# Layer 0's attention to the context: keys and values projected in the self-attention before it, batches in a pipeline

## The chip, the cores and the metric

One core of a Trainium2 chip runs the whole program. Its engines work from queues of their own, each in order: TensorE (PE; its weight loads are listed as PEld), VectorE (DVE), ScalarE (ACT), GpSimd (POOL) and SyncE (SP, which here only starts transfers). The metric is the device time of one execution in microseconds; the time before is 2743.05 us, the median of three runs (2738.83 to 2749.72).

## What is computed

The reference is a decoder of four layers on 8 batches of 256 tokens with 256 features, each layer made of a part that mixes the tokens (in layer 0 a self-attention), an attention to a context (8 batches of 120 rows with 192 features) and a feed-forward part, each followed by an addition and a layer norm. The parts of the first three layers stand one after the other in the list `LAYERS`; the fourth layer is run from inside the third's feed-forward part, and the change does not touch it. Only these lines of the reference matter here:

```python
x = _layernorm(x + _L0_attn_ref(x, ...))
x = _layernorm(x + _L0_xattn_ref(x, ctx_768, Wq, bq, Wk, bk, Wv, bv))

def _L0_xattn_ref(image_features, text_features, Wq, bq, Wk, bk, Wv, bv):
    query = jnp.einsum('bqi,ih->bqh', image_features, Wq) + bq
    key = jnp.einsum('bkt,th->bkh', text_features, Wk) + bk
    value = jnp.einsum('bkt,th->bkh', text_features, Wv) + bv
    scale = 1.0 / jnp.sqrt(jnp.asarray(HID, query.dtype))
    scores = jnp.einsum('bqh,bkh->bqk', query, key) * scale
    weights = jax.nn.softmax(scores, axis=-1)
    return jnp.einsum('bqk,bkh->bqh', weights, value)
```

The attention to the context has one head of 256 features and no output projection. Its keys and values depend on the context alone, so they do not wait for the self-attention.

## The kernel before

`Net` keeps the tokens in `X` (128 tokens per tile, 16 tiles, two per batch), a transposed copy in `xT` (features on the partitions), and the transposed context in `ctxT`. `build` runs the parts in order, and loads each part's weights one part ahead: `load` (L120, L124) takes one of two slots in turn, and starts the transfers on SP's queue. A part's slot is therefore free for the load after the next only when that part is through with it. The program's instructions are placed on the engines' queues by a scheduler which may move them past each other where the data allow it; on the chip each queue then runs in its order.

`l0_attn` works in turns of `t`, 0 to 7. In each turn `exps` and `largest` make score products in four banks at a time (`four_banks`, mask L443, scores L448), `lower16` turns the row maxima (L500) and writes them into the queries (L502), `sums` multiplies the exponentials with the values (L275), and `divided16` divides. Every even turn `pair` projects queries, keys and values of the next two. All of it takes PSUM banks from one rotation of eight (`bank`): six of the pool `sc`, then the two of the transposes, `pt`. After the turns, `project_out` runs for the eight batches: product with `wo` (L134), addition (L292), then `finish`: statistics on VectorE (L165, L166), the reciprocal root on GpSimd (`rsqrt`, L143 and L145, since `power` is set for this part), X on VectorE (L189), and four transposes with a copy on ScalarE back into `xT` (L175, L176).

`l0_xattn` opens pools of its own and projects first: keys for all 960 context rows (`project_T`, evicted at L334), queries for all 2048 tokens (the same lines, scaled by 1/16), values per batch with the bias as a third product (L136) and a copy on ScalarE (L360). Then it runs over 8 batches with two halves each: score product, negative row maximum (L371), exponential with its sum (L374), reciprocal (L375), transpose of the weights into `pt` (L377), its copy (L379), product with the values, division and addition in one (L382). `finish` closes the batch.

`l0_ffn` comes next. It makes the router's 32 small products with `xT` (`plog`), copies them (L827), finds each token's expert, writes X to memory (L877, on ScalarE's queue; the scheduler starts each write as soon as its X is there), and then gathers the experts' weights and rows.

A product in 32-bit floats shows as two rows, called passes here, each with a weight load of its own.

Of the kernel before, what the change touches and what calls it, by code (L numbers as in the profile page):

```python
# [11 lines left out]
F32 = mybir.dt.float32  # L12
# [30 lines left out]
class Net:  # L43
# [169 lines left out]
    def l0_attn(self, w):  # L213
# [3 lines left out]
        nc = self.nc  # L217
        wq, wk, wv, wo, bv, bo = w
        rows = [slice(32 * r, 32 * r + 32) for r in range(4)]
        of = [slice(0, P), slice(P, 2 * P)]  # L220
        xs = self.xT.rearrange("p c (g n) -> p c g n", n=P)
        with ExitStack() as ctx:
            work, low, vps = self.attn16_pools(ctx, "a0", P, 2)
            pool = ctx.enter_context(self.tc.tile_pool(name="a0a", bufs=1))
            aT = pool.tile([P, 2, NTOK], F32, name="aT")
            bv, bo = self.everywhere(bv, work, "bv"), self.everywhere(bo, work, "bo")
            groups = aT.rearrange("p c (n g) -> p c g n", g=16)
            other = self.other.unsqueeze(1).to_broadcast([P, 4, P])
            q, k = {}, {}

            def pair(t):
                src = xs[:, :, 2 * t : 2 * t + 4, :]
                qv, kv = (work.tile([P, 2, 2, 512], F32, name=name) for name in ("qv", "kv"))
                self.project16(qv, wq, src, self.col("l0a_bq"), 512, "q")
                self.project16(kv, wk, src, self.col("l0a_bk"), 512, "k")
                for n in range(4):
                    pv = self.bank([P, 512])[:, :D]
                    self.mm(pv, [(src[:, c, n, :], wv[:, c, :]) for c in range(2)])
                    self.values16(vps[t // 2 % 2][:, n // 2, n % 2, :], pv, P, bv)
                for n in range(2):  # L240
                    q[t + n], k[t + n] = (v[:, :, :, n * S : (n + 1) * S] for v in (qv, kv))

            def largest(t, j):
                low5 = low[t % 2][:, j].rearrange("p m (r u w) -> p r m u w", u=2, w=16)
                self.four_banks(
                    [P, 4, P],
                    (lambda sc: sc, other),
                    lambda r: [
                        (2 * m + u, q[t][rows[r], u, m, of[j]], k[t][rows[r], u, m, of[j]])
                        for m in range(2) for u in range(2)  # L250
                    ],
                    lambda r, sc: nc.vector.tensor_reduce(low5[:, r, :, :, 0], sc, AX.X, ALU.max, negate=True),
                )

            def exps(t, m):
                e = work.tile([P, 4, 2, 2, P], F32, name="e0")
                self.four_banks(
                    [P, 4, P],
                    (lambda sc: sc, other),
                    lambda r: [  # L260
                        (2 * u + j, k[t][rows[r], u, m, of[j]], q[t][rows[r], u, m, of[j]])
                        for u in range(2) for j in range(2)
                    ],
                    lambda r, sc: nc.scalar.activation(e[:, r].rearrange("p u j n -> p (u j) n"), sc, AF.Exp),
                )
                return e

            def sums(t, es):
                for m in range(2):
                    av = self.bank([P, 2, 2, P])  # L270
                    for u in range(2):
                        for j in range(2):
                            for r in range(4):
                                o = 16 * (1 - u) + (4 * m + r) * 48
                                nc.tensor.matmul(  # L275
                                    av[rows[r], u, j, :], lhsT=vps[t // 2 % 2][:, t % 2, j, o : o + 32],
                                    rhs=es[m][:, r, u, j, :], start=True, stop=True, skip_group_check=True,
                                )
# [39 lines left out]
    def project_T(self, dst, w, src, n, ps, bias=None, scale=1.0):  # L318

        nc = self.nc  # L320
        kc = w.shape[1]
        k = 0
        for m in range(dst.shape[1]):
            for o in range(0, n, 512):
                e = min(o + 512, n)
                pp = ps.tile([P, 512], F32, name="pp")
                self.mm(pp[:, : e - o], [(w[:, c, m * P : (m + 1) * P], src[:, c, o:e]) for c in range(kc)])
                if bias is None:
                    if k % 2:
                        nc.scalar.mul(dst[:, m, o:e], pp[:, : e - o], scale)  # L330
                    else:
                        nc.vector.tensor_scalar(dst[:, m, o:e], pp[:, : e - o], scale, None, ALU.mult)
                else:
                    nc.vector.tensor_scalar(  # L334
                        dst[:, m, o:e], pp[:, : e - o], bias[:, m : m + 1], scale, ALU.add, ALU.mult
                    )
                k += 1

    def l0_xattn(self, w):
        nc, tc = self.nc, self.tc  # L340
        wq, wk, wv, bv = w
        with (
            tc.tile_pool(name="x0", bufs=1) as pool,
            tc.tile_pool(name="x0w", bufs=3) as work,
            tc.tile_pool(name="x0p", bufs=2, space=PSUM) as ps,
        ):
            kT = pool.tile([P, 2, NCTX], F32, name="kT")
            self.project_T(kT, wk, self.ctxT, NCTX, ps, self.col("l0x_bk"))
            qT = pool.tile([P, 2, NTOK], F32, name="qT")
            self.project_T(qT, wq, self.xT, NTOK, ps, self.col("l0x_bq"), D**-0.5)  # L350
            v = pool.tile([SC, B, D], F32, name="v")
            for b in range(B):
                pv = ps.tile([P, 512], F32, name="pp")
                self.mm(
                    pv[:SC, :D],
                    [(self.ctxT[:, c, b * SC : (b + 1) * SC], wv[:, c, :]) for c in range(2)],
                    bias=bv,
                    m=SC,
                )
                nc.scalar.copy(v[:, b, :], pv[:SC, :D])  # L360
            for b in range(B):
                z = work.tile([P, 2, D], F32, name="z")
                for j in range(2):
                    i = 2 * b + j
                    psc = ps.tile([P, SC], F32, name="psc")
                    self.mm(
                        psc,
                        [(qT[:, c, i * P : (i + 1) * P], kT[:, c, b * SC : (b + 1) * SC]) for c in range(2)],
                    )
                    nm = work.tile([P, 1], F32, name="nm")  # L370
                    nc.vector.tensor_reduce(nm, psc, AX.X, ALU.max, negate=True)  # L371
                    e = work.tile([P, SC], F32, name="e")
                    sm = work.tile([P, 1], F32, name="sm")
                    nc.scalar.activation(e, psc, AF.Exp, bias=nm, accum_out=sm)  # L374
                    nc.vector.reciprocal(sm, sm)  # L375
                    pt = self.ps_t.tile([SC, P], F32, name="pt")
                    nc.tensor.transpose(pt, e, self.ident)  # L377
                    eT = work.tile([SC, P], F32, name="eT")
                    nc.scalar.copy(eT, pt)  # L379
                    pa = ps.tile([P, 512], F32, name="pp")  # L380
                    self.mm(pa[:, :D], [(eT, v[:, b, :])])
                    nc.vector.scalar_tensor_tensor(z[:, j], pa[:, :D], sm, self.X[:, i, :], ALU.mult, ALU.add)  # L382
                self.finish(2 * b, 1, z)

# [1760 lines left out]
```

## Time and profile before

| What | us |
|---|---|
| median of three runs | 2743.05 |
| the profiled execution, its own time | 2746.13 |
| its span, first to last instruction | 2744.3 |
| TensorE, VectorE, ScalarE, GpSimd busy | 2185.0, 1629.2, 986.4, 934.9 |
| first product of the self-attention's projections starts | 21.9 |
| last X of the self-attention's norm | 204.9 to 205.6 |
| first scores of the attention to the context (psc) | 237.66 |
| its last z (L382) ends | 289.2 |
| logits of the router copied (L827) | 304.9 to 305.2 |

The parts around the change fill the first 305 us of the span; all later parts stay as they are. The page's busy shares are means over the whole span. A stage of a few ten microseconds is read from the rows of a window, where the busy time of each engine and the granted clock of TensorE stand side by side (1.00 is full speed).

### The profile page before, as it was taken

Reading aid. Unit: us, or ns where it says so; the run is one execution under the profiler, and the core shown is the slowest. Engines: PE = TensorE matmul, PEld = TensorE weight load, DVE = VectorE, ACT = ScalarE, POOL = GpSimd, SP = SyncE. Lnnn points to the kernel's source line nnn. Section 1 sums busy time; section 2 is a strip of 40 time slices with the busy share of each in tenths; the row PEclk is TensorE's granted clock in tenths of the full one; section 3 lists DMA queues with packets and bytes.
Section 4 is the critical chain, followed back from the end, with each engine's and each line's share of the span. In section 5 each row is a group of like instructions: output and inputs, shape, how many; then the busy total and the mean of one; then the engine's idle time right before and its main releaser. Section 6 shows DMA issues by size and latency. Waiting matters only on the chain.

```text
span 2744.3 us, 41139 instructions
## 1 busy us (share of the span) xinstructions
PE 2185.0 (80%) x14461; PEld 1577.9 (57%) x14461; DVE 1629.2 (59%) x5582; ACT 986.4 (36%) x2237; POOL 934.9 (34%) x980
## 2 busy tenths in 40 slices
PE   8978689699988879757885667778887778777796
PEld 5555578645565558534454246556666666555575
DVE  4663300276667676235667886657676676655675
ACT  2322133234333442113342243334444344343563
POOL 1020121221111124443210036665565654663122
PEclk9998599899988779878998888888898898887898
DMA  2001233200010027511001011111111111220000
GB/s 82 2 1 43 106 135 123 70 9 2 1 62 17 18 85 225 163 52 32 16 1 58 1 61 46 41 49 39 41 45 35 53 38 35 56 73 19 0 13 19
DMA packets 84173, 135.05 MB, mean 49 GB/s; under 512 B 33445, under 2 KB 53045, under 8 KB 82048
## 3 DMA queue, kind: packets, MB, share of 16 engines
q0 software_dynamic: 52288, 79.27, 9.9%
q1 hardware_dynamic: 28924, 49.45, 5.4%
q10 hardware_dynamic: 2756, 3.72, 0.4%
q8 instruction: 115, 1.88, 0.3%
q14 instruction: 90, 0.74, 0.1%
HBM read 242.90 MB, written 17.70 MB: 95 GB/s over the span
## 4 chain that ended last, share of the span: by engine, by line
PE 37%; DVE 21%; issue 9%; POOL 5%; ACT 4%; DMA 3%; another core or an unknown queue 3%; POOLq 0%; ACTq 0%; DVEq 0%
PE po L1464 5%; PE pp L134 5%; PE s L134 4%; PE sc L134 4%; DVE low L481 2%; PE ph L134 2%; PE sc L448 2%; PE pt L134 2%; DMA xe<-xd,take 2%; DVE low L465 2%; PE sc L569 1%; DVE junk L1412 1%; POOL w L919 1%; DVE X L189 1%
## 5 line engine op out<-in xcount | busy, mean ns | idle before, releaser
L919 POOL DMA_INDIRECT rows<-in_l2f_table_dram,index x512 | 531.4, 1038 | 354.9 <-issue 125.2
L1464 PE MATMUL po<-rows,diag 128*128 128x256 f32 x768 | 232.4, 439 | 80.3 <-ACT diag L1463 44.8
L1412 DVE SCALAR_TENSOR_TENSOR junk<-rows,X 128x256 f32<-128x256 f32 x512 | 214.1, 418 | 60.6 <-DMA rows<-in_l2f_table_dram,index 30.6
L1464 PEld LDWEIGHTS po<-rows,diag 128*128 128x128 f32 x768 | 154.5, 215 | 132.1 <-ACT diag L1463 59.6
L134 PE MATMUL pp<-xT,w 128*128 128x256 f32 (+1 forms) x672 | 196.9, 435 | 37.1 <-issue 22.5
L134 PE MATMUL ph<-xeT,we 128*128 128x128 f32 x1248 | 180.6, 287 | 20.5 <-DMA we<-in_l0f_experts_dram,wrow 15.6
L134 PEld LDWEIGHTS ph<-xeT,we 128*128 128x128 f32 x1248 | 166.5, 197 | 41.3 <-DMA we<-in_l0f_experts_dram,wrow 17.1
L556 POOL TENSOR_TENSOR aT<-sides,inv 128x256 f32<-128x256 f32 x64 | 46.8, 731 | 419.3 <-DVE sides L554 238.6
L134 PEld LDWEIGHTS pp<-xT,w 128*128 128x128 f32 x672 | 141.2, 217 | 72.2 <-issue 32.2
L1463 ACT ACTIVATE diag<-ident,dots 128x128 f32<-128x128 f32 x384 | 134.7, 394 | 128.2 <-PE po L1464 50.5
L175 PE MATMUL pt<-ident,X 128*128 128x128 f32 x352 | 77.5, 333 | 116.9 <-DVE X L189 99.0
L176 ACT COPY xT<-pt 128x512 f32<-128x512 f32 x88 | 51.6, 586 | 293.1 <-PE pt L175 248.0
L919 POOL DMA_INDIRECT xe<-xd,take x87 | 85.4, 981 | 203.4 <-DVE y L1040 78.6
L175 PEld LDWEIGHTS pt<-ident,X 128*128 128x128 f32 x352 | 49.7, 164 | 150.6 <-DVE X L189 60.7
L134 PE MATMUL py<-we,hT 128*128 128x256 f32 x496 | 129.3, 385 | 0.9 <-DVE hT L1063 0.9
L1040 DVE TENSOR_TENSOR y<-py,we 128x256 f32<-128x256 f32 x23 | 9.8, 425 | 196.0 <-PE py L134 196.0
L520 ACT ACTIVATE e<-sc 128x512 f32<-128x512 f32 (+1 forms) x154 | 81.4, 602 | 103.2 <-PE sc L448 74.4
L1034 ACT ACTIVATE hT<-ph,we 128x128 f32<-128x128 f32 x184 | 65.5, 367 | 118.0 <-PE ph L134 84.9
L448 PE MATMUL sc<-kv,qv 32*128 32x128 f32 (+2 forms) x1448 | 103.5, 320 | 1.7 <-DVE qv L666 0.6
L448 PEld LDWEIGHTS sc<-kv,qv 32*128 32x128 f32 x1448 | 79.9, 190 | 32.7 <-issue 26.4
L189 DVE TENSOR_SCALAR X<-z,ln_mv,rs_y 128x256 f32<-128x256 f32 x176 | 66.1, 418 | 52.2 <-POOL rs_y L145 51.8
L448 PE MATMUL sc<-qv,kv 32*128 32x128 f32 (+2 forms) x1384 | 97.0, 343 | 0.1
(509 smaller groups left out, 5188.9 us busy)
## 6 DMA issues: line engine op xcount, KB each, us to landing
we<-in_l1f_experts_dram SPq DMA_DIRECT2D x32, 384.0 KB
yd<-y SPq DMA_DIRECT2D x32, 256.0 KB
rows<-in_l2f_table_dram,index POOLq DMA_INDIRECT x512
w<-in_l2x_w_dram SPq DMA_DIRECT2D x1, 4096.0 KB
yd<-y SPq DMA_DIRECT2D x23, 128.0 KB
X<-in_x_dram SPq DMA_DIRECT2D x8, 256.0 KB
xd<-X ACTq DMA_DIRECT2D x8, 256.0 KB
xd<-X SPq DMA_DIRECT2D x8, 256.0 KB
```

Of the source, the lines that this page charges most:

```text
L134: self.nc.tensor.matmul(out, lhsT=lhsT, rhs=rhs, start=n == 0, stop=n == last and bias is None)
L175: nc.tensor.transpose(pt[:, c, j, :], self.X[:, i0 + j * step, c * P : (c + 1) * P], self.ident)
L189: nc.vector.tensor_scalar(self.X[:, i, :], z[:, j, :], mv[:, j, 0:1], r[:, j : j + 1], ALU.subtract, ALU.mult)
L448: nc.tensor.matmul(sc[: shape[0], part], lhsT=lhsT, rhs=rhs, start=mask is None, stop=True, skip_group_check=True)
L465: nc.vector.tensor_reduce(low5[:, r, :, :, 0], sc, AX.X, ALU.max, negate=True)
L481: nc.vector.tensor_reduce(low4[:, r, :, 0], sc, AX.X, ALU.max, negate=True)
L520: lambda r, sc: nc.scalar.activation(e0[m][:n0, r], sc, AF.Exp),
L919: self.nc.gpsimd.indirect_dma_start(out=out, out_offset=None, in_=table, in_offset=bass.IndirectOffsetOnAxis(ap=index, axis=0), **({} if r ...
L1034: nc.scalar.activation(hT[:, g + f, :], ph[:, f, :], AF.Gelu, bias=b1[:, g + f : g + f + 1])
L1412: nc.vector.scalar_tensor_tensor(junk, row, 1.0, self.X[:, i, :], ALU.mult, ALU.mult, accum_out=out)
L1463: nc.scalar.activation(diag, self.ident, AF.Copy, scale=dots[:, k : k + 1])
L1464: nc.tensor.matmul(po, lhsT=diag, rhs=rows[:, k, D:], start=False, stop=g + k == H * K - 2)
```

## The change

Keys and values of layer 0's attention to the context are projected in the turns of the self-attention before it, two batches of keys each even turn and one batch of values each turn, in banks of the same rotation. They are kept in the weights' slot (`spare`), so that they outlive the self-attention's pools. The values' bias is broadcast once over the partitions (`everywhere`), and added where the values are evicted, now on VectorE; the keys are evicted on ScalarE. `l0_xattn` keeps only the queries, per pair of batches, split between ScalarE and VectorE, and runs as a pipeline: scores of batch b + 1 and queries of the pair after are issued ahead of the sums of batch b, and the transposes into `xT` of batch b - 1 after them. Both halves of a batch share one tile for the scores, the maxima, the exponentials and the transposed weights, which have a bank of their own (`pe`).

```diff
@@ l0_attn
+            cwk, cwv, cbv, kT, v = self.ctx0
+            cbv = self.everywhere(cbv, work, "cbv")
+            def context(b):
+                if b % 2 == 0:
+                    ctxT = self.ctxT[:, :, b * SC : (b + 2) * SC]
+                    pk = self.bank([P, 2, 256])[:, :, : 2 * SC]
+                    for m in range(2):
+                        self.mm(pk[:, m, :], [(cwk[:, c, m * P : (m + 1) * P], ctxT[:, c, :]) for c in range(2)])
+                        nc.scalar.activation(
+                            kT[:, m, b * SC : (b + 2) * SC], pk[:, m, :], AF.Identity,
+                            bias=self.col("l0x_bk")[:, m : m + 1],
+                        )
+                pv = self.bank([P, 512])[:SC, :D]
+                self.mm(pv, [(self.ctxT[:, c, b * SC : (b + 1) * SC], cwv[:, c, :]) for c in range(2)])
+                nc.vector.tensor_tensor(v[:, b, :], pv, cbv[:SC], ALU.add)
...
                     self.lower16(q[t + 1], low[(t + 1) % 2])
+                context(t)
                 sums(t, es)
@@ load_l0_xattn
-        return self.load(("l0x_wq", 2), ("l0x_wk", 2), ("l0x_wv", 2), rows=("l0x_bv",))
+        *w, spare = self.load(
+            ("l0x_wq", 2), ("l0x_wk", 2), ("l0x_wv", 2), rows=("l0x_bv",), spare=2 * NCTX + B * D
+        )
+        kT = spare[:, : 2 * NCTX].rearrange("p (c n) -> p c n", c=2)
+        v = spare[:SC, 2 * NCTX :].rearrange("p (b d) -> p b d", b=B)
+        self.ctx0 = w[1], w[2], w[3], kT, v
+        return w[0], kT, v
@@ l0_xattn
-            kT = pool.tile([P, 2, NCTX], F32, name="kT")
-            self.project_T(kT, wk, self.ctxT, NCTX, ps, self.col("l0x_bk"))
-            self.project_T(qT, wq, self.xT, NTOK, ps, self.col("l0x_bq"), D**-0.5)
-            v = pool.tile([SC, B, D], F32, name="v")
...
+            def queries(b):
+                for m in range(2):
+                    o = b * S
+                    pp = ps.tile([P, 2, D], F32, name="pp").rearrange("p j d -> p (j d)")
+                    self.mm(pp, [(wq[:, c, m * P : (m + 1) * P], self.xT[:, c, o : o + 512]) for c in range(2)])
+                    if m:
+                        nc.vector.tensor_scalar(
+                            qT[:, m, o : o + 512], pp, D**-0.5, bq[:, m : m + 1], ALU.mult, ALU.add
+                        )
+                    else:
+                        nc.scalar.activation(
+                            qT[:, m, o : o + 512], pp, AF.Identity, bias=bq[:, m : m + 1], scale=D**-0.5
+                        )
+            def scores(b):
+                psc = ps.tile([P, 2, SC], F32, name="psc")
+                for j in range(2):
+                    o = b * S + j * P
+                    self.mm(
+                        psc[:, j, :],
+                        [(qT[:, c, o : o + P], kT[:, c, b * SC : (b + 1) * SC]) for c in range(2)],
+                    )
...
+                nc.vector.tensor_reduce(nm, psc, AX.X, ALU.max, negate=True)
...
+                for j in range(2):
+                    nc.scalar.activation(
+                        e[:, j, :], psc[:, j, :], AF.Exp, bias=nm[:, j : j + 1], accum_out=sm[:, j : j + 1]
+                    )
...
+            def sums(b, e, sm):
+                pt = ps.tile([SC, 2, P], F32, name="pe", bufs=1)
+                for j in range(2):
+                    nc.tensor.transpose(pt[:, j, :], e[:, j, :], self.ident)
...
+                nc.scalar.copy(eT, pt)
...
+                for j in range(2):
+                    self.mm(pa[:, j, :], [(eT[:, j, :], v[:, b, :])])
+                    nc.vector.scalar_tensor_tensor(
+                        z[:, j], pa[:, j, :], sm[:, j : j + 1], self.X[:, 2 * b + j, :], ALU.mult, ALU.add
+                    )
-                self.finish(2 * b, 1, z)
+                self.finish_x(2 * b, 1, z)
+            def turn(b):
+                self.transpose_into_xT(2 * b, 1)
+            queries(0)
+            ready = scores(0)
+            for b in range(B):
+                here = ready
+                if b % 2 == 0 and b + 2 < B:
+                    queries(b + 2)
+                if b + 1 < B:
+                    ready = scores(b + 1)
+                sums(b, *here)
+                if b:
+                    turn(b - 1)
+            turn(B - 1)
```

More of the change, by code (lines that the diff above doesn't have):

```diff
@@ L315, in load_l0_xattn @@
     def load_l0_xattn(self):
-        return self.load(("l0x_wq", 2), ("l0x_wk", 2), ("l0x_wv", 2), rows=("l0x_bv",))
[L318 to L337, printed above, removed]
+        *w, spare = self.load(
[5 more added lines that the diff above has]
+        return w[0], kT, v
     def l0_xattn(self, w):
         nc, tc = self.nc, self.tc
-        wq, wk, wv, bv = w
+        wq, kT, v = w
         with (
@@ L346, in l0_xattn @@
         ):
-            kT = pool.tile([P, 2, NCTX], F32, name="kT")
-            self.project_T(kT, wk, self.ctxT, NCTX, ps, self.col("l0x_bk"))
             qT = pool.tile([P, 2, NTOK], F32, name="qT")
-            self.project_T(qT, wq, self.xT, NTOK, ps, self.col("l0x_bq"), D**-0.5)
-            v = pool.tile([SC, B, D], F32, name="v")
[L352 to L360, printed above, removed]
@@ L361, in l0_xattn @@
-            for b in range(B):
+            bq = pool.tile([P, 2], F32, name="bq")
+            nc.vector.tensor_scalar(bq, self.col("l0x_bq"), D**-0.5, None, ALU.mult)
+            def queries(b):
[11 more added lines that the diff above has]
+                        )
@@ new lines, in scores @@
+            def scores(b):
[6 more added lines that the diff above has]
+                    )
+                nm = work.tile([P, 2], F32, name="nm")
+                nc.vector.tensor_reduce(nm, psc, AX.X, ALU.max, negate=True)
+                e = work.tile([P, 2, SC], F32, name="e")
+                sm = work.tile([P, 2], F32, name="sm")
+                for j in range(2):
+                    nc.scalar.activation(
+                        e[:, j, :], psc[:, j, :], AF.Exp, bias=nm[:, j : j + 1], accum_out=sm[:, j : j + 1]
+                    )
+                nc.vector.reciprocal(sm, sm)
+                return e, sm
@@ L362, in l0_xattn @@
+            def sums(b, e, sm):
+                pt = ps.tile([SC, 2, P], F32, name="pe", bufs=1)
+                for j in range(2):
+                    nc.tensor.transpose(pt[:, j, :], e[:, j, :], self.ident)
+                eT = work.tile([SC, 2, P], F32, name="eT")
+                nc.scalar.copy(eT, pt)
+                pa = ps.tile([P, 2, D], F32, name="pp")
                 z = work.tile([P, 2, D], F32, name="z")
                 for j in range(2):
-                    i = 2 * b + j
-                    psc = ps.tile([P, SC], F32, name="psc")
@@ L366, in l0_xattn @@
-                    self.mm(
-                        psc,
-                        [(qT[:, c, i * P : (i + 1) * P], kT[:, c, b * SC : (b + 1) * SC]) for c in range(2)],
-                    )
[L370 to L382, printed above, removed]
```

## The prediction

> **What bounds the kernel now.** The page's engine shares (TensorE 80%, VectorE 59%) average stages with different limits, so I read the busy time of each engine in stretches cut at this layer's stage boundaries, then the waits of TensorE in the first stretch, then the timeline of one late batch. In the first view the columns are the stretch, its length, each engine's busy time (instructions), the granted TensorE clock, DMA share and GB/s.
>
> ```profile
> core 0: us, PE busy (x) PEld busy (x) DVE busy (x) ACT busy (x) POOL busy (x), PEclk, DMA share, GB/s
> 21.90:167.50 145.60, 136.99 (x1824) 86.07 (x1824) 97.18 (x213) 51.81 (x95) 11.05 (x15) 1.00 0.01 2
> 167.50:201.60 34.10, 20.73 (x88) 15.63 (x88) 17.64 (x53) 3.41 (x6) 14.22 (x21) 0.84 0.01 1
> 201.60:237.70 36.10, 36.10 (x106) 18.10 (x105) 11.22 (x20) 4.36 (x10) 1.44 (x3) 0.96 0.00 1
> 237.70:289.30 51.60, 35.72 (x142) 24.36 (x141) 23.54 (x91) 15.08 (x56) 6.49 (x14) 0.68 0.20 67
> 289.30:305.20 15.90, 14.93 (x68) 14.46 (x69) 1.92 (x11) 0.84 (x2) 1.23 (x3) 0.50 0.05 18
> ```
>
> The rows are: scores and sums of the self-attention; its output projection with the layer norms; the projections for the attention to the context; its eight batches; the router's 32 small products up to the copy of the logits. TensorE has 137.0 of 145.6 us in the first and all of the third. The fourth has no busy engine: VectorE 23.5 of 51.6 us, ScalarE 15.1, TensorE 35.7, and that at a clock of 0.68. The timeline (start, duration, engine, line) shows why:
>
> ```profile
> 277.21 0.48 PE L175 MATMUL pt<-ident,X 128*128 128x128 f32 x1 [1.59 <-DVE X L189]
> ...
> 278.58 0.59 ACT L176 COPY xT<-pt 128x512 f32<-128x512 f32 x1 [3.30 <-PE pt L175]
> 279.06 0.27 ACT L379 COPY eT<-pt 120x128 f32<-120x128 f32 x1
> ...
> 279.48 1.98 PE L134 MATMUL pp<-v,eT 120*128 120x256 f32 x4
> ...
> 280.65 0.48 DVE L382 SCALAR_TENSOR_TENSOR z<-pp,sm,X 128x256 f32<-128x256 f32 x1 [3.17 <-PE pp L134]
> ...
> 282.95 0.22 POOL L143 TENSOR_SCALAR rs_v<-ln_mv 128x2 f32<-128x2 f32 x1 [6.24 <-DVE ln_mv L166]
> ...
> 284.00 0.74 DVE L189 TENSOR_SCALAR X<-z,ln_mv,rs_y 128x256 f32<-128x256 f32 x2 [1.14 <-POOL rs_y L145]
> 284.46 0.18 PEld L175 LDWEIGHTS pt<-ident,X 128*128 128x128 f32 x1 [3.73 <-DVE X L189]
> ```
>
> One turn is 277.21 to 284.46, 7.25 us. The next batch's weights stand ready, yet their copy (eT) stands on ScalarE behind the xT copy of the batch before, which stands behind its layer norm: a ring of queue order, not of data.
>
> **The changed parts, on the profiled execution** (2746.13 us, span 2744.3; 3.1 us above the median of 2743.05).
>
> (1) *Keys and values into the self-attention.* Added to TensorE: keys, 4 pairs x 2 halves x 2 chunks x 2 passes = 32 passes of 240 columns. A 512-column pass of this kind repeats every 0.43 us in the trace (the weight loads at 212.36, 212.79, 213.22), so 240/512 x 0.43 = 0.20 each, 6.4 us. Values, 32 passes of 256 columns at 0.21, 6.8 us. The broadcast bias, two passes at the start, 0.6 us (its row is loaded right behind the other rows, which waited until 15.42 us; in the built order it stands behind the eight transposes, so no new wait). Sum 13.8 us. Gone for good are the 16 bias passes: a batch of values took 1.67 us (start to start, 225.95 to 227.62), of which four passes are about 0.95.
>
> What hides them? TensorE's waits in that stretch are these (waiting row, releaser, total, times, longest):
>
> ```profile
> PE sc L500 <- DVE low L252: 2.8, 6, 0.6
> PE pt L443 <- DVE sides L554: 2.1, 2, 1.0
> PE sc L443 <- DVE sides L554: 2.1, 2, 1.0
> PE pt L500 <- DVE low L252: 0.9, 2, 0.4
> ```
>
> In the built order the new products stand between the first and the second of the four transposes of L500, so they fill part of these 3.7 us, which the weighted sums filled before; I let them cover 2.3. Here the Trainium skill advises ("Perfetto Trace Analysis", Optimization Strategy) interleaving regimes whose most-contended engines differ. That speaks against this half of the change: TensorE work goes into the stretch where TensorE is the contended engine, and by the rule nothing is hidden, 13.8 us; by the row 11.5. I take **+11.5** (ends +8, all waits filled and some bubbles too, and +17, new bank waits). The evictions (8 key copies on ScalarE and 8 value additions on VectorE, about 0.4 us each by the 256-column rows at L360 and L433) lie beside it: ScalarE has 94 us free there, VectorE 48. If that cover failed they would cost 6.4 us. What is queued behind: the second half's key product waits for the copy of the first half (one PSUM tile), and that copy waits on ScalarE behind eight exponentials (0.6 us each); TensorE has about 3.7 us of its own work in between, so no stall.
>
> (2) *The output projection.* Thirteen more banks are claimed, which turns the eight-bank rotation: before, batches 4 and 5 have the two transpose banks (pt), now 0 and 7. Batch 7's product then waits for batch 6's transposes, where batch 4's waited before. I take **-1** (ends -6, 0).
>
> (3) *The projection stretch.* Before, the last X is done at 205.6 and the first scores start at 237.66. After, the first pair's queries (8 passes, 3.4 us) lie in the gaps of the output projection, and the first scores follow the last transposes, about 0.9 us after X. So the first scores start at 205.6 + 11.5 - 1 + 0.9 = 217.0: **20.7 us earlier**.
>
> (4) *The batches.* TensorE at full clock: the remaining queries 24 x 0.43 = 10.3; scores 64 passes at 0.14 (eight in 1.15 us) 9.2; sums 32 x 0.21 = 6.8; 16 transposes of e and 28 of X about 6.5. Sum 33. VectorE: 23.5, less 1.2 for eight reduces fewer, plus 3 x 0.75 for queries, 25. ScalarE about 20. I walked the built order with these durations, all queues in order, from the first scores at 0: second queries done at 4.9, first X at 13.9 (scores two batches ahead fill TensorE meanwhile), last queries at 26, then X of batch 4 at 33, of 5 at 38, last z at 39.5. Up to 26 TensorE is nearly full, after it the chain z - statistics - GpSimd - X shows again, but with two batches in flight. ScalarE's eight xd writes are issued behind X, so each blocks ScalarE until its X is there; this is in the walk. I add 2.5 for a TensorE that starts at half clock: **42 us instead of 51.6, -9.6** (ends 36 and 60).
>
> (5) *The clock.* The skill ("TensorE: Matmul & The Clock Gate", Part 1) has TensorE at half clock after one idle window of about 3.4 us and at full clock after as long a busy one. By it the eight batches would have stayed warm (longest TensorE wait 3.0 us), and the router's 12 us of gapless products would warm up: 6 us saved in the tail of both kernels. The trace disagrees: 0.68 and 0.50. So I leave the tail at its 15.9 us and take **-1** for the chance that it is entered warm (by the rule alone -6).
>
> (6) *The weights of layer 1's attention.* kT and v now live in their slot, so SP can issue these six loads (1.5 MB, L120, issued from 237.8 us until now) only when the batches are through with them, and SP's queue waits there. Behind them are loads used much later and the first expert's result; layer 1's attention starts after 500 us. Cost 0; without that cover, 5 us.
>
> Sum: -20.7 - 9.6 - 1 = -31.3, so 2714.8 in this execution's terms. The profiled execution stands 3.1 us above the median, so against the median **2712 us**.
>
> **The rivals.**
> *Cold pipeline.* The batches start from a stage at half clock (0.50 to 0.60 between 190 and 205 us) and their small products may keep it there; 33 us of TensorE work become 60 or so: -20.7 + 8.4 = -12, 2731. For it: in 237.7 to 289.3 TensorE was 69% busy and went cold. Against: its first 26 us are denser, and the gapless projections ran at 1.00.
> *Banks, the slower side.* Each context turn claims one or two banks of the rotation ahead of the sums, so the four-bank score rounds (32 in the stretch) may land on banks whose reader is late. At 1.5 us a round it is +48, with the rest -31: 2760. It decides from 1.0 us a round. Against: all waits on banks there (L443) were 4.2 us.
> *Nothing to gain.* Both at a third of their strength, about 2743: the same time.
> *More.* The tail warm, and the self-attention's bubbles filled: -48, 2695.
>
> **How the numbers follow.** Forecast (saving 20 to 45 us) 0.75; cold pipeline 0.12; more 0.04; nothing 0.05; banks 0.04. A measurement of this kernel can tell 0.5%, 13.7 us, from no change; about half of the cold case falls inside it. So faster 0.86, same 0.09, slower 0.05. The range takes the bounds of (1) and (4): low 2695 (warm tail, +8, 36), high 2731 (the cold case).
>
> **What would show it.** The context products at about 0.2 us a pass in 22 to 180 us, and the self-attention's sums ending near 179; the first psc near 217; X spaced 5 us or less; z of the last batch near 259; logits near 274; nothing changed after but the shift. It would be wrong if TensorE's waits before L477 (the mask products) grow, or if the clock in the batches stays 0.5.

## The result and the profile after

The changed kernel takes 2702.27 us (median of four runs, 2698.26 to 2706.66). A fourth run of the kernel before, beside it, makes that kernel's median 2740.94: 38.7 us less between the medians. The ratio of the runs to those of before is given as 0.9846, with a 95% interval from 0.9813 to 0.9879; it is not the quotient of the two medians, which is 0.9859. The profiled execution has a span of 2696.5 us.

The first view is again the busy time in stretches, now cut at the changed kernel's own marks: scores and sums with the context products in them; the output projection; the piece up to the first scores (psc); the eight batches; the router. The columns are those of the same view above.

```profile
21.60:173.30 151.70, 147.53 (x1889) 95.12 (x1888) 100.07 (x219) 55.70 (x104) 10.32 (x14) 1.00 0.01 2
173.30:210.40 37.10, 25.29 (x101) 17.52 (x101) 22.25 (x63) 4.72 (x9) 16.32 (x24) 0.91 0.01 1
210.40:211.50 1.10, 0.65 (x5) 0.32 (x4) 0.96 (x3) 0.74 (x2) 0.00 (x0) 1.00 0.00 0
211.50:250.70 39.20, 35.41 (x164) 23.56 (x164) 24.62 (x79) 14.60 (x50) 6.47 (x14) 0.94 0.13 42
250.70:266.70 16.00, 14.98 (x70) 14.47 (x69) 1.77 (x11) 1.44 (x3) 1.23 (x3) 0.50 0.36 129
```

The projection stretch of 32 us has shrunk to 1.1. TensorE is busy in 35.4 of the batches' 39.2 us (35.7 of 51.6 before), at a clock of 0.94 instead of 0.68. The router is as it was: 16 us at 0.50.

The second view is TensorE's waits in the first stretch:

```profile
PE sc L534 <- DVE low L252: 1.8, 6, 0.6
PE sc L477 <- DVE sides L588: 1.4, 3, 0.6
PE pt L477 <- DVE sides L588: 0.6, 1, 0.6
PE pt L534 <- DVE low L252: 0.4, 2, 0.2
```

They add up to 4.2 us, where the four rows of before in the prediction add up to 7.9. The third is the timeline of a late batch:

```profile
236.32 0.74 DVE L189 TENSOR_SCALAR X<-z,ln_mv,rs_y 128x256 f32<-128x256 f32 x2 [1.13 <-POOL rs_y L145]
...
237.24 0.60 PE L175 MATMUL pt<-ident,X 128*128 128x128 f32 x4
237.50 0.37 ACT L395 COPY eT<-pe 120x256 f32<-120x256 f32 x1 [1.52 <-PE pe L393]
...
237.88 0.59 ACT L176 COPY xT<-pt 128x512 f32<-128x512 f32 x1
237.92 0.70 PE L134 MATMUL pp<-w,eT 120*128 120x256 f32 x2
...
242.28 0.74 DVE L189 TENSOR_SCALAR X<-z,ln_mv,rs_y 128x256 f32<-128x256 f32 x2 [0.78 <-POOL rs_y L145]
```

The copy of the weights (eT) now comes ahead of the copy into `xT` on ScalarE, and the products with the values no longer wait for the norm of the batch before. (The two X shown are the widest pair, with the last queries between them; the spacing in the eight batches is 2.0 to 6.0 us, where before it was 5.9 to 7.2.)

**A fixed point to count from.** The first mask product of the self-attention starts at 33.22 us in the trace of before, at 32.06 in that of after, and between 32.1 and 36.1 in the fourteen traces of this study. Two things differ there, and neither follows the change: the first projections start between 21.6 and 23.4 us, and up to seven of their first passes take 0.85 us or more where the later ones take 0.43. That looks like half clock, though the clock column reads 1.00 in that place (its records begin only at 20 to 29 us). At the other end, the time from the logits to the end of the span lies between 2430 and 2453 us, in kernels that share nearly all of that code. So the spans (47.8 us apart here) scatter by more than most parts of this change are worth. I count every mark from the first mask product; counted so, the last sums start at 133.4 in four of the five kernels without context products among them, and at 133.9 in the fifth.

| from the first mask product, us | last sums | last X done | first psc | last z done | logits copied |
|---|---|---|---|---|---|
| before | 133.4 | 172.4 | 204.4 | 256.0 | 271.7 |
| after | 140.9 | 178.4 | 179.4 | 218.6 | 234.3 |
| pipe_only | 133.4 | 174.4 | 197.3 | 234.8 | 250.5 |
| ctx_only | 140.9 | 177.3 | 177.7 | 242.2 | 257.9 |
| claims_only | 133.4 | 169.8 | 188.5 | 226.0 | 241.7 |
| before_fill | 133.4 | 174.0 | 206.0 | 254.1 | 269.8 |
| ctx_in_outproj | 133.9 | 180.7 | 181.7 | 219.3 | 235.0 |
| router_early | 140.9 | 177.3 | 178.3 | 220.4 | 226.5 |
| router_warm | 140.9 | 177.3 | 178.3 | 216.0 | 230.7 |
| pe_in_pt | 140.9 | 178.3 | 179.4 | 220.1 | 235.4 |
| six_banks | 140.9 | 174.5 | 177.4 | 214.8 | 230.5 |
| both | 140.9 | 174.5 | 175.8 | 218.8 | 224.9 |
| context_twice | 153.9 | 190.6 | 191.6 | 229.2 | 244.9 |
| queries_first | 140.9 | 178.1 | 191.3 | 221.4 | 235.1 |

"Last sums" is the start of the last product of L275, and "logits copied" the start of the copy. The change is worth 37.4 us at the logits.

### The profile page after: what moved, and what is told of

Same layout as the page of the kernel before. It is cut to its first block, busy times and chain, and to the rows that moved or that the text cites. A ratio compares the mean times of both kernels' runs of the same rounds, so it can differ in the third digit from the quotient of the medians.

```text
span 2696.5 us, 41126 instructions
## 1 busy us (share of the span) xinstructions
PE 2157.2 (80%) x14463; PEld 1564.6 (58%) x14463; DVE 1624.2 (60%) x5567; ACT 987.7 (37%) x2234; POOL 935.2 (35%) x980
## 4 chain that ended last, share of the span: by engine, by line
PE 36%; DVE 22%; issue 10%; POOL 5%; ACT 4%; DMA 3%; another core or an unknown queue 3%; POOLq 0%; ACTq 0%; DVEq 0%
PE po L1498 5%; PE pp L134 4%; PE sc L134 4%; PE s L134 4%; DVE low L515 2%; DMA xe<-xd,take 2%; PE ph L134 2%; PE sc L482 2%; PE pt L134 2%; DVE low L499 2%; PE sc L603 2%; DVE junk L1446 1%; POOL rows L953 1%; DVE X L189 1%
## 5 line engine op out<-in xcount | busy, mean ns | idle before, releaser
L1446 DVE SCALAR_TENSOR_TENSOR junk<-rows,X 128x256 f32<-128x256 f32 x512 | 214.8, 420 | 53.4 <-DMA rows<-in_l2f_table_dram,index 32.4
L1497 ACT ACTIVATE diag<-ident,dots 128x128 f32<-128x128 f32 x384 | 134.3, 395 | 117.8 <-PE po L1498 48.1
L176 ACT COPY xT<-pt 128x512 f32<-128x512 f32 x88 | 51.6, 586 | 271.6 <-PE pt L175 232.4
L175 PEld LDWEIGHTS pt<-ident,X 128*128 128x128 f32 x352 | 49.9, 164 | 140.3 <-DVE X L189 51.6
## 6 DMA issues: line engine op xcount, KB each, us to landing
yd<-y SPq DMA_DIRECT2D x32, 256.0 KB
X<-in_x_dram SPq DMA_DIRECT2D x8, 256.0 KB
xd<-X ACTq DMA_DIRECT2D x8, 256.0 KB
xd<-X SPq DMA_DIRECT2D x8, 256.0 KB
```

What stands on the lines that cost most here:

```text
L175: nc.tensor.transpose(pt[:, c, j, :], self.X[:, i0 + j * step, c * P : (c + 1) * P], self.ident)
L1446: nc.vector.scalar_tensor_tensor(junk, row, 1.0, self.X[:, i, :], ALU.mult, ALU.mult, accum_out=out)
L1497: nc.scalar.activation(diag, self.ident, AF.Copy, scale=dots[:, k : k + 1])
```

## The experiments

My theory was the prediction's: the projections leave the stretch of their own and cost less in the self-attention, and the pipeline breaks a ring that comes from the order of the queues. The main rival was that the slow batches were slow because of the clock.

### The two halves apart

**pipe_only** keeps the pipeline and takes the context out of the self-attention.

```diff
-                context(t)
                 sums(t, es)
...
+            self.project_T(kT, cwk, self.ctxT, NCTX, ps, self.col("l0x_bk"))
+            for b in range(B):
+                pv = ps.tile([P, 2, D], F32, name="pp").rearrange("p j d -> p (j d)")
+                self.mm(
+                    pv[:SC, :D],
+                    [(self.ctxT[:, c, b * SC : (b + 1) * SC], cwv[:, c, :]) for c in range(2)],
+                    bias=cbv,
+                    m=SC,
+                )
+                nc.scalar.copy(v[:, b, :], pv[:SC, :D])
             queries(0)
             ready = scores(0)
```

> The pipeline alone: keys and values are projected at the start of the attention to the context, not in the self-attention. Theory (the two halves of the change add up): last sums of the self-attention at 166.9 us and its last X at 205.6, as before; about 19.9 us of key and value products (keys 6.5, values 8 x 1.67) stand ahead of the first scores, so these start near 225; then the same eight batches as in the changed kernel, 39 us, last z at 264, logits copied at 280, 24 to 25 us earlier than before. Rival (the halves lean on each other, because queries fill gaps that the keys and values now fill): batches over 43 us, logits after 284.

Its batches took 37.5 us, and its logits came 21.2 us before the old kernel's (ratio 0.9900, 0.9866 to 0.9934). The rival's mark (over 43) was missed: the queries had room enough. The logits at 285.5 on the trace's own clock are later than the 280 I wrote, since this run began 1.9 us late and spent 22.9 us between last X and first psc.

**ctx_only** is the reverse: the changed self-attention, and the old loop over the batches with all queries asked for ahead of it.

> The other half alone: keys and values in the self-attention, the old loop over the batches with all queries ahead of it. Theory (parts add up, ring of queue order): last sums at 173.3, last X at 210.4; 13.8 us of query products, most of them behind that X, so first scores at 220 to 223; batches 51 us as before with a clock that falls to about 0.7; logits near 288, 16 us earlier than before. Rival (the clock was the cause of the slow batches, and a shorter stage ahead changes it): batches of 42 us, logits near 279.

The logits came 13.8 us earlier (ratio 0.9951, 0.9933 to 0.9969). One expectation failed by its mark: the first psc came right behind the last X, at 212.5 us, because the scheduler put scores ahead of most of the queries. So the batches' stretch holds the queries:

```profile
212.50:277.10 64.60, 48.29 (x163) 31.32 (x161) 27.44 (x97) 15.34 (x56) 6.49 (x14) 0.64 0.09 29
```

This is the changed context with the old ring behind it: 48 us of TensorE work at a clock of 0.64. The halves give 21.2 + 13.8 = 35.0 of the 37.4 us, so they nearly add.

### Products or banks: what the self-attention pays

**claims_only** is pipe_only with the thirteen claims of the rotation, but nothing in them:

```diff
+            self.bank([P, 512])
             pair(0)
...
+                if t % 2 == 0:
+                    self.bank([P, 512])
+                self.bank([P, 512])
                 sums(t, es)
```

> As pipe_only, but the self-attention claims the thirteen extra banks of the rotation without any product in them. It parts the 6.4 us that the self-attention became longer into products and bank order. Theory A (the new products cost 6.4 us because they fill waits and bubbles; the turned rotation costs and gives nothing): last sums at 166.9 plus or minus 0.7. Theory B (the turned rotation itself gives some us): last sums at 161 to 164, so that the products cost 9 to 12. The output projection, too: its length from last sums to last X is 38.7 before and 37.1 in the changed kernel; by theory it is 37 here, from the banks.

Theory A: 133.4, as without claims. The turned rotation is free in the self-attention, and the products cost 7.5 us there. Behind it the rotation does matter. From last sums to last X it takes 39.0, 41.0 and 40.6 us in the three kernels with the old rotation (before, pipe_only, before_fill), and 36.3 to 37.4 in the eight with the new one and nothing else changed in that stage: 3.5 us less in the mean. (The clock there was 0.77 to 0.83 with the old rotation and 0.91 to 1.00 with the new one. Whether the banks gave all of it directly, or part of it by way of the clock, these runs do not show.) Between claims_only and pipe_only the logits differ by 8.8 us: 4.7 of them in this stage, the rest in the projections behind it (18.8 us instead of 22.9).

**context_twice** makes each context product twice:

```diff
                     for m in range(2):
-                        self.mm(pk[:, m, :], [(cwk[:, c, m * P : (m + 1) * P], ctxT[:, c, :]) for c in range(2)])
+                        for _ in range(2):
+                            self.mm(pk[:, m, :], [(cwk[:, c, m * P : (m + 1) * P], ctxT[:, c, :]) for c in range(2)])
...
-                self.mm(pv, [(self.ctxT[:, c, b * SC : (b + 1) * SC], cwv[:, c, :]) for c in range(2)])
+                for _ in range(2):
+                    self.mm(pv, [(self.ctxT[:, c, b * SC : (b + 1) * SC], cwv[:, c, :]) for c in range(2)])
```

> The changed kernel with each product of keys and values in the self-attention made twice (the second overwrites the first). By their rates (0.20 and 0.21 us a pass) the 64 passes are 13.3 us, but the stretch from the first mask product to the last sums grew only by 7.5, from 133.4 to 140.9. Theory A (waits and bubbles hid about 6 us, and are used up): the second dose costs 12 to 13.5, last sums at 153 to 154.5. Theory B (such a pass costs only 0.12 us among others): 7.5 again, last sums at 148 to 149. Between them: part of the room is left.

153.9: the second dose cost 13.0 us, nearly the full price of its passes (13.3), and the listed waits stayed at 4.6 us (4.2 with one dose). So the first dose was not cheap work; some 6 us of it went into room that is now used up.

### Order or clock: what the batches gain

**before_fill** is the kernel before with eight products per batch that nobody reads, so that TensorE has work all the time:

```diff
-                self.finish(2 * b, 1, z)
+                self.finish_x(2 * b, 1, z)
+                fill = ps.tile([P, 4, P], F32, name="fill", bufs=1)
+                for _ in range(8):
+                    nc.tensor.matmul(
+                        fill, lhsT=self.ident_bf, rhs=self.other.unsqueeze(1).to_broadcast([P, 4, P]),
+                        start=True, stop=True, skip_group_check=True,
+                    )
+                self.transpose_into_xT(2 * b, 1)
```

> The kernel before, with eight products of 512 columns per batch added to its loop whose results nobody reads, only to keep TensorE busy between the batches. It asks what part of the 51.6 us of the batches was the clock (0.68) and what part the order of the queues. Theory (order): the clock rises above 0.9, but one turn of the ring stays near 6.4 us, because only about 1.3 us of PE time in it is halved: batches of 46 to 50 us. Rival (clock): batches of 38 to 42 us, as in the changed kernel. If the clock stays below 0.8, the fill did not do what it was for.

```profile
238.50:286.60 48.10, 38.30 (x206) 24.30 (x205) 23.58 (x91) 14.84 (x56) 6.49 (x14) 0.94 0.21 72
```

The clock is that of the changed kernel, 0.94, and the batches still take 48.1 us. The timeline shows the same ring at full clock; in order X, transposes, copy into `xT`, copy of the weights, products, next X:

```profile
263.21 0.73 DVE L189 TENSOR_SCALAR X<-z,ln_mv,rs_y 128x256 f32<-128x256 f32 x2 [0.91 <-POOL rs_y L145]
...
264.69 0.59 ACT L176 COPY xT<-pt 128x512 f32<-128x512 f32 x1 [1.85 <-PE pt L175]
265.18 0.27 ACT L379 COPY eT<-pt 120x128 f32<-120x128 f32 x1
...
265.50 1.21 PE L134 MATMUL pp<-v,eT 120*128 120x256 f32 x4
...
269.25 0.73 DVE L189 TENSOR_SCALAR X<-z,ln_mv,rs_y 128x256 f32<-128x256 f32 x2 [0.78 <-POOL rs_y L145]
```

One turn is 6.04 us instead of 7.25; the products take 1.21 instead of 1.98. The clock is therefore worth about 3.5 us of the batches, and the new loop the rest. (The fill itself stands in TensorE's queue, so 3.5 is a lower bound.) The new loop is more than a new order: it also joins the two halves of a batch in one tile, so that there is one row maximum and one copy of the weights per batch instead of two. No run takes the joining alone, and its share of the rest stays open.

**queries_first** keeps the pipeline but asks for all queries ahead of the first scores:

```diff
-            queries(0)
+            for b in range(0, B, 2):
+                queries(b)
             ready = scores(0)
...
-                if b % 2 == 0 and b + 2 < B:
-                    queries(b + 2)
```

> The changed kernel with all queries asked for ahead of the first scores, as before, the pipeline otherwise kept. Theory (the queries are what fills TensorE's waits in the first half of the pipeline): the first scores come 6 to 10 us later (24 passes of 0.43 us, some in gaps of the output projection), batches become 32 to 36 us instead of 39.2, logits 3 to 6 us later than the changed kernel, at 237 to 240 from the first mask product. Rival (the chain of each batch sets the pipeline, queries or not): batches stay at 37 to 39, logits at 241 to 244.

The batches took 30.1 us:

```profile
227.00:257.10 30.10, 24.78 (x137) 18.84 (x135) 21.59 (x74) 12.02 (x46) 5.55 (x12) 0.89 0.16 53
```

This is the comparison like for like with the old 51.6, since both have no queries in them: the pipeline saves 21.5 us on the same work, and 18.0 against before_fill, whose clock was about as high. The first psc came 11.9 us later, more than the 6 to 10 expected, and yet the logits only 0.7 us later, less than expected. The batches gave back 9.1 us of that, and the router 2.0: the clock happened to rise just before the router began (0.58 in that stretch instead of 0.50). Without that luck the logits would be about 2.7 us later. Where the queries stand matters little: TensorE does the same work either ahead of the batches or among them.

**pe_in_pt** gives the transposed weights the banks of the X transposes again (`pt = self.ps_t.tile([SC, 2, P], F32, name="pt")`).

> The changed kernel, but the transposed weights share the two banks of the transposes of X again, as before. Theory A (the bank of its own is what breaks the ring; without it the weights' transposes wait for the copies of X): batches 44 to 50 us instead of 39.2. Theory B (scores a batch ahead and transposes a batch behind break it): batches 38 to 42 us.

40.7 us instead of 39.2: theory B. The bank of its own is worth about 1.5 us; it does not break the ring.

### Work put into the waits

**ctx_in_outproj** moves the context products to where TensorE waits most:

```diff
-                context(t)
                 sums(t, es)
...
             for b in range(B):
+                context(b)
                 project_out(b)
```

> The changed kernel, but each batch's keys and values are projected in front of that batch's output projection, where TensorE waits 12 to 13 us for layer norms, and not in the turns of scores and sums, where it hardly waits. Counted from the first mask product of the self-attention (the changed kernel: last sums 140.9, last X 178.3, logits 234.3). Theory (work put into waits is nearly free, and it keeps the clock up): last sums back at 133.4, the stage from last sums to last X 37 to 41 us instead of 37.4, logits at 227 to 231, 3 to 7 us before the changed kernel. Rival (its products stand in front of the chain product - norm - transposes, and its evictions on VectorE and ScalarE between the norms, so that each batch is later): that stage 45 us or more, logits at 234 or later.

The rival came true. The sums ended 7.1 us earlier, and the stage behind became 46.8 us instead of 37.4; the logits stand at 235.0, no better than 234.3. Two rows of the waits in that stage (the waiting engine, tile and line, whom it waits for, total, times, longest), first of the changed kernel:

```profile
PE pt L175 <- DVE X L189: 10.1, 6, 2.8
DVE z L292 <- PE pt L134: 6.1, 2, 3.3
```

and of ctx_in_outproj:

```profile
PE pt L175 <- DVE X L189: 7.1, 8, 1.4
DVE z L292 <- PE pt L134: 7.1, 3, 3.9
```

TensorE's wait for X shrank by only 3 us, though 13 us of work were added, and VectorE waits longer for projections, which now stand behind context products in TensorE's queue. The waits of this stage are the far side of a chain (product, addition, norm, X, transposes); what stands in front of one of its products makes the chain itself later. How much of the 9.4 us is that, the run does not show, because it also changes the banks: by the trace, three output projections and two value products of this stage now take a transpose bank, where the changed kernel has two output projections on them. The next run shows what two alone cost.

**six_banks** leaves the work and changes the banks of the output projection:

```diff
+            self.banks = self.banks[:6] + self.banks[:2]
             for b in range(B):
                 project_out(b)
```

> The changed kernel, but the output projections take their banks from the six of the scores alone, never from the two of the transposes. Counted from the first mask product. Theory (a batch whose product has a transpose bank waits for the copy into xT two batches back, and that wait, not the norms, sets the stage): the stage from last sums to last X 29 to 34 us instead of 37.4 (VectorE has 22 us in it), logits at 226 to 231 instead of 234.3. Rival (the chain of norm, GpSimd and X sets it with any banks): 36 to 38 us, logits at 233 to 235.

The stage took 33.6 us instead of 37.4, inside the expected 29 to 34, at the same clock (0.91), and the logits came at 230.5. VectorE's waits for products in a transpose bank (6.1 us above) are gone, and TensorE's wait for X is 7.9 us instead of 10.1:

```profile
PE pt L175 <- DVE X L189: 7.9, 6, 1.6
```

So a part of this stage's length was never the norms: it was a product that waited for a transpose bank. Only 2.1 us of it reach the first scores, since part of the first queries then stand behind the last X. (The batches behind it took 37.5 us instead of 39.2; in pipe_only, claims_only, ctx_in_outproj and context_twice they took 37.4 to 37.5, so the other 1.7 us at the logits are not this edit's alone.)

### The router

**router_early** issues the router's products of a batch behind its transposes, in the bank that the pipeline leaves free:

```diff
             def turn(b):
                 self.transpose_into_xT(2 * b, 1)
+                for i in (2 * b, 2 * b + 1):
+                    self.mm(plog[:, i, :], [(self.xT4[:, c, i, :], self.gate0[:, c, :]) for c in range(2)])
...
```

The rest of the edit opens `plog` ahead of the pipeline and takes the same products out of `l0_ffn`.

> The changed kernel with the router's products of a batch issued right behind that batch's transposes, into a bank of their own, inside the pipeline. Counted from the first mask product. Theory (the 15.7 us tail of 64 thin products runs at half clock only because it stands alone): 56 of the products take 0.12 us each in the pipeline, batches 41 to 45 us instead of 39.2, and only the last eight stand behind it: logits at 224 to 229 instead of 234.3. Rival (thin products bring the clock down wherever they stand): clock in the batches below 0.8, batches 48 us or more, logits at 231 or later.

The logits came at 226.5, 7.8 us earlier, of which 1.1 came before the batches. These took 42.1 us at a clock of 0.97:

```profile
211.70:253.80 42.10, 39.79 (x216) 28.54 (x216) 25.38 (x80) 15.54 (x51) 6.49 (x14) 0.97 0.13 44
```

From the last z to the logits it took 6.1 us instead of 15.7. **router_warm** instead keeps TensorE busy up to the router with 16 products that nobody reads:

```diff
...
+            fill = ps.tile([P, D], F32, name="fill", bufs=1)
+            for n in range(16):
+                self.mm(fill, [(eT[:, n % 2, :], v[:, B - 1, :])])
```

> The changed kernel with 16 products of 256 columns, read by nobody, in the gaps of the last batch, so that TensorE enters the router's products without an idle stretch behind it. Theory (by this case's traces, thin products do not count as work for the clock): it starts at 1.00 and falls to 0.50 within some 4 us, logits at 232 to 236 from the first mask product (the changed kernel: 234.3). Rival (the clock falls only when TensorE is idle): 1.00 throughout, 64 products at 0.12 us, logits at 229 to 231.

The measured 230.7 lies with the rival's times, but the mechanism is the theory's: of the 3.6 us only 1.0 was won from the last z on (14.7 us instead of 15.7), and the rest before it. The stretches of 2 us (the router's products start at 256.83):

```profile
256.00:258.00 2.00, 2.00 (x19) 1.90 (x17) 0.38 (x5) 0.47 (x1) 0.30 (x1) 1.00 0.28 81
258.00:260.00 2.00, 2.00 (x21) 2.00 (x20) 0.00 (x0) 0.12 (x1) 0.00 (x0) 1.00 0.98 326
260.00:262.00 2.00, 2.00 (x16) 2.00 (x15) 0.00 (x0) 0.00 (x0) 0.00 (x0) 0.72 0.93 327
262.00:264.00 2.00, 2.00 (x11) 2.00 (x10) 0.00 (x0) 0.00 (x0) 0.00 (x0) 0.50 0.33 127
```

TensorE has no gap, and yet some 4 us after the products of 8 columns begin its clock falls to half: of the 63 steps between the starts of its 64 passes the first 37 are 0.11 us or less, the other 26 are 0.21. The loads for layer 1 run at the same time here (DMA share 0.98), but the old kernel's router stood at 0.50 with a DMA share of 0.05, so they are not needed to hold it there; whether they helped to bring it down, this run cannot say.

**both** joins router_early and six_banks.

> router_early and six_banks together. Theory (the two gains lie in different stages and add): router_early had logits at 226.5 from the first mask product; with the shorter output projection 219 to 223, and the whole kernel 0.25 to 0.5% below router_early, a ratio to the kernel before of 0.977 to 0.981. Rival (the pipeline behind starts colder or has fewer gaps for its first queries): logits at 225 or later, ratio 0.982 or more.

The logits came at 224.9, only 1.6 us before router_early and later than the 219 to 223 expected: the output projection ended 2.8 us earlier, but its batches took 43.0 us. It has the earliest logits of all, 9.5 us before the changed kernel. In the whole time that cannot be shown: the ratios to the kernel before are 0.9836 (0.9808 to 0.9863) for both, 0.9836 (0.9800 to 0.9871) for six_banks, 0.9823 (0.9791 to 0.9856) for router_early and 0.9846 (0.9813 to 0.9879) for the changed kernel. That a version beats the changed kernel in total stays open.

## Why the prediction was right, step by step

Counted from the first mask product, the prediction's sum of 31.3 us became 37.4 at the logits; of the whole, 31 us were forecast between the medians and 38.7 measured. The forecast case happened, and all its large steps were right in kind. The term with the largest error of its own is the cover in step 1. The errors lie nearly all on one side, so the sum is not right by cancelling. (The low end's own terms, a warm tail, +8 and 36, add up to 2697, not 2695.)

1. *Keys and values into the self-attention, +11.5.* Measured +7.5, below the low end of 8. The price of the passes was right (the second dose in context_twice cost 13.0; I had 13.8 with the bias). The mis-sized term is the cover: I let the products fill 2.3 us of the waits, and about 6 went. The listed waits shrank by 3.7 (7.9 to 4.2); where the other 2 us went no row lists. Bubbles between products of different kinds are a guess. The rule of the Trainium skill that I weighed here ("Perfetto Trace Analysis", Optimization Strategy: interleave regimes whose most-contended engines differ), as I read it, would have given +13.8, further off; the rule itself gives no cost. ctx_in_outproj put the work where TensorE is less busy (25.3 of 37.1 us instead of 147.5 of 151.7), and its stage grew by 9.4 us instead of 7.5, the changed banks included.
2. *The output projection, -1.* Measured -1.6 in the two traces (39.0 to 37.4), -3.5 between the groups of traces. The mechanism (turned rotation) is shown by claims_only and six_banks; I had its size too small.
3. *The first scores 20.7 us earlier.* 25.0 earlier, which is steps 1 and 2 again (4.0 and 0.6), and 1.1 us from last X to psc, about as I had it (0.9).
4. *Batches of 42 us.* 39.2. The walk through the queues gave 39.5, and first X at 13.9 (measured 12.7), X of batch 4 at 33 (30.8), last z at 39.5 (39.2). The 2.5 us added for a cold start was not needed. The cold start itself was there: five kernels with the same batches took 37.4 to 37.5 us at clocks of 0.98 to 1.00, where the changed kernel has 0.94. So the walk, which had no cold start in it, was about 2 us too long, and that it met 39.2 is luck. ScalarE had 14.6 us and not the "about 20" of the prediction; nothing hung on it. X was not spaced by 5 us or less everywhere: at the widest it was 6.0, where the queries stand between.
5. *The clock in the tail, -1.* 0: from last z to logits 15.7 us before and after. Leaving the tail alone was right. By the rule of the Trainium skill ("TensorE: Matmul & The Clock Gate", Part 1) the router's gapless products should have warmed the clock; router_warm shows that a queue full of such products does not even keep it up.
6. *Weights of layer 1 later, 0.* These loads are now issued at 249.3 to 251.9 us instead of behind 237.8. From the logits to the end took 2436 us in the mean of the two kernels with early loads and 2439 in that of the nine with late loads whose router stands as before, each scattering by several us. No cost can be seen.

Of the rivals, the cold pipeline did not come (0.94); the banks on the slower side did not either (waits ahead of the mask products fell from 4.2 to 2.0 us). The profiled spans differ by 47.8 us, 9 more than the medians; that part lies behind the logits, in the scatter described above.

## What to carry to other kernels

A stretch in which no engine is busy is worth more than a stretch in which one is: before moving work, look whether its length comes from a queue that holds a ready instruction behind a wait of another batch. Idle time of an engine need not be room for more work, since the idle can be the latency of a chain through that engine; test that before moving work into it, for the stage that looked full here took the same work for no more than the one that was a third idle. And the list of waits is not a bound on what a full stretch hides: here some 2 us more vanished than the waits shrank by, and the second dose of the same work was paid nearly in full.

## What was not expected of the hardware

Products of 8 columns keep TensorE's queue full and its clock low: it ran at 0.50 through the whole router, and fell from 1.00 to 0.50 some 4 us after wider products had ended (router_warm), while the same products between wide ones left it at 0.97 (router_early). The old batches show the other half of it: their clock fell from 1.00 (240 to 250 us) to 0.50 (255 to 260 us) though no wait of TensorE there was longer than 3.0 us. And the first mask product moves by up to 4 us from trace to trace, by when the first projections start and by how many of their first passes take double time.
